# Loading a later block's x at the head of a block's steps instead of beside its row scatters

## The chip, the cores and the metric

The kernel runs on one core of a Trainium2 chip. Its time is the device time of one execution in microseconds; the time before is the median of three runs. Below, TensorE (PE) is the matrix engine, VectorE (DVE) and ScalarE (ACT) are the elementwise engines, GpSimd (POOL) issues indirect DMAs here, and SyncE (SP) issues plain DMAs. All DMAs are carried by the same 16 DMA engines of the core.

## The reference

The input x has 2 sequences of 4096 rows, 256 wide, in 32-bit floats. Two layers follow each other, both with a residual and a layer norm behind them.

```python
# layer 0: retention
q = (x @ Wq.T);  v = (x @ Wv.T)
state[t] = lam * state[t - 1] + v[t]          # along the sequence, lam by head
y = layernorm(q * state) * ln_g + ln_b
x = layernorm(x + (y * silu(x @ Wg.T)) @ Wo.T)
# layer 1: two of eight experts for each row
gates = softmax(x @ gate_W);  top two, scaled to sum 1 -> cw
out = x + sum_e cw[:, e] * (relu(x @ W1[e] + b1[e]) @ W2[e] + b2[e])
x = layernorm(out)
```

## The kernel before

The 8192 rows are taken in 16 blocks of 512 (`NB`). A block i passes through `attention(i)`, a generator whose `yield`s cut it into twelve steps: transposes of x, the projections v (with the scan that gives the state), g and q, the norm of y, the output product with the residual, the first layer norm (`x1`), the transposes of x1, the routing, and last the row scatters.

In the row scatters (L505) GpSimd issues eight indirect DMAs. Each sends 128 rows of x1, with their weights and row numbers, to a table `xs` in device memory that is ordered by expert, so that each row stands there twice. `schedule` then plans slots: 256 rows of one expert each, four for most blocks.

A slot is worked off in stages. `load_slot` (L605, SyncE) reads its rows as the tile xg. `slot_weights` (L619, L621, ScalarE) copies the expert's weights from `kept`. `slot_columns` (L632 on TensorE, L633 on VectorE) transposes xg. `slot_first` (L645 `ph`, L652 `hT`) and `slot_second` (L666 `po`, then L674 to L684 on VectorE, which make `to`, `weight` and `ysl`) are the two expert products. `store_slot` (L692, GpSimd) scatters the result rows to a table `ys`. When all slots of a group of blocks are stored, `load_sum` (L714) reads `ys` back, `weigh`, `scale_of` and `end` add the pairs and normalise, and `write_out` (L754) stores the output.

The two groups are 13 and 3 blocks long. The order of the instructions on TensorE, VectorE, ScalarE and SyncE is the order in which the program is written out (`IN_ORDER`), so it is set by the main loop (L836). In its turn i the loop advances the generators of blocks i - 2 (`older`), i - 1 (`old`), i (`new`) and i + 1 (`after`, its first step alone, the transposes of x_{i+1}). Between these steps `fill(n)` puts in slot work (`half`), loads of slots ahead (`load_ahead`, at most three) and, in turns 0 and 1, the loads of the experts' weights (`keep`, four DMAs an expert). The last `next(older)` of a turn holds the row scatters of block i - 2.

`load_x(i)` (L99 to L102) asks SyncE to load 512 KB into a tile of the ring `x` of five buffers. x_0 to x_2 are loaded at the start, x_{i+2} in turn i. The ring's buffer for x_{i+2} held x_{i-3}, which is read for the last time in turn i - 2 (L403). SyncE's queue is in order: a load of xg that waits for a free buffer (four of them, freed by L684) holds everything behind it.

Of the kernel before, what the change touches and what calls it, by code (L numbers as in the profile page):

```python
# [30 lines left out]
def kernel(  # L31
# [31 lines left out]
    NB = B * L // TB  # L63
# [27 lines left out]
    def wide_tile(name):  # L91
        wide_done.append(False)
        t = work.tile([P, NT, D], FP, tag="x", name=name, bufs=WIDE)
        return t, len(wide_done) - 1
# [4 lines left out]
    def load_x(i):  # L99
        t, k = wide_tile(f"x_{i}")  # L100
        nc.sync.dma_start(out=t, in_=xb[i])
        x_tiles[i] = t, k  # L102
# [42 lines left out]
    def keep(e, after):  # L145
        dma = nc.sync.dma_start(
            out=w2_sb[:, e, :, :], in_=w2[e].rearrange("(c p) d -> p c d", p=P)
        )
        if after is not None:
            tc.add_manual_dep(dma.ins, after, SYNC, reason="not all at once")  # L150
        at = 0
        for src, n in (
            (w1[e].rearrange("(c p) f -> p c f", p=P), NC),
            (b2[e : e + 1].partition_broadcast(P), 1),
            (b1[:, ts(e, NF)].unsqueeze(1), 1),
        ):
            size = n * src.shape[-1]
            nc.sync.dma_start(
                out=kept[:, e, at : at + size].rearrange("p (c f) -> p c f", c=n), in_=src
            )  # L160
            at += size
# [604 lines left out]
    def load_ahead():  # L766
        while slots and len(loaded) + len(ready) + len(turned) < 3:
            loaded.append(load_slot(slots.pop(0)))

    def turn_ahead():  # L770
        if not turned:
            weights_ahead()
        if ready and not turned:
            turned.append(slot_columns(ready.pop(0)))
# [21 lines left out]
    def half():  # L796

        turn[0] ^= 1
        done, size = 0, P
        if turn[0] or not hidden:  # L800
            load_ahead()
            turn_ahead()
            if turned:
                size = done = turned[0][4]
                weights_ahead()
                hidden.append(slot_first(turned.pop(0)))
        if not done and (len(hidden) == 2 or (hidden and not turned and not slots)):
            size = done = hidden[0][4]
            out_of.append(slot_second(hidden.pop(0)))
        elif out_of:  # L810
            store_slot(out_of.pop(0))
        load_ahead()
        turn_ahead()
        if not any(left.values()):
            return done

        todo = 3 * len(to_load) + len(to_weigh)
        debt[0] += todo * size / (P * max(1, 2 * sum(left.values()) - 8))
        some_combining(int(debt[0]))
        debt[0] -= int(debt[0])  # L820
        return done
# [14 lines left out]
    for i in range(NB + 2):  # L836

        now = sum(s[4] for s in slots + loaded) + sum(s[4] for s in ready + turned)
        now = 2 * min(5 * SL, now - SL * LAG * (i > FEW))

        def fill(n):
            nonlocal now
            if to_keep:
                keep(to_keep.pop(0), projected[0])
            load_ahead()
            for _ in range(n):
                done = 0
                while now > 0 and done < SL:
                    size = half() or SL
                    done += size  # L850
                    now -= size

        older, old, new, after = (
            steps[j] if 0 <= j < NB else iter(()) for j in (i - 2, i - 1, i, i + 1)
        )
        next(old, None)
        next(new, None)
        next(older, None)
        next(old, None)
        fill(1 if i > FEW else 0)  # L860
        next(new, None)
        next(old, None)
        if now > 0:
            turn_ahead()
        next(older, None)
        fill(1)
        next(new, None)
        fill(1)
        next(old, None)
        if 0 < i < NB - 2:  # L870
            load_x(i + 2)
        next(after, None)
        next(older, None)
        fill(1)
        next(old, None)
        fill(10)
# [57 lines left out]
```

## Time and profile before

| what | us |
|---|---|
| median of 3 runs | 1092.39 |
| lowest and highest run | 1091.66, 1093.06 |
| the profiled execution | 1088.11 |
| its span, first to last instruction | 1086.4 |
| TensorE busy in the span | 914.8 |
| VectorE busy | 623.1 |
| ScalarE busy | 389.7 |
| GpSimd busy | 339.7 |

The profile is of one execution. A page gives each engine's busy share in 40 slices of the span; with it go the clock that TensorE was granted (in tenths of full speed) and the busy share of the DMA engines. Other views list who waited for whom, the chain of waits that ended last, and the instructions of an engine in order of time; there, a number in brackets is the idle time before a row and the arrow names what ended it. "remote" and "another core or an unknown queue" stand where the profile finds no instruction that ended a wait in time. Queue q0 holds GpSimd's DMAs, q1 SyncE's, q8 and q14 the instruction fetches.

The x loads are issued at 0.9, 1.4, 2.0, 52.9, 54.3, 54.8, 124.7, 164.0, 232.4, 302.0, 356.9, 419.0, 476.5, 531.4, 588.9 and 643.2 us. The first transposes that read x_i start at 5.1, 33.2, 50.4, 76.0, 107.9, 143.2, 180.0, 238.3, 292.7, 347.5, 409.7, 467.1, 522.1, 579.5, 633.9 and 693.0 us. Row scatters of a block start at 80.6, 112.4, 147.9, 184.7, 243.0, 297.3, 352.2, 414.4, 471.8, 526.8, 584.2, 638.6, 697.7, 755.7, 810.0 and 856.8 us and take 9 to 10 us.

### The profile page before, as it was taken

Reading aid. Unit: us, or ns where it says so; the run is one execution under the profiler, and the core shown is the slowest. Engines: PE = TensorE matmul, PEld = TensorE weight load, DVE = VectorE, ACT = ScalarE, POOL = GpSimd, SP = SyncE. Lnnn points to the kernel's source line nnn. Section 1 sums busy time; section 2 is a strip of 40 time slices with the busy share of each in tenths; the row PEclk is TensorE's granted clock in tenths of the full one; section 3 lists DMA queues with packets and bytes.
Section 4 is the critical chain, followed back from the end, with each engine's and each line's share of the span. In section 5 each row is a group of like instructions: output and inputs, shape, how many; then the busy total and the mean of one; then the engine's idle time right before and its main releaser. Section 6 shows DMA issues by size and latency. Waiting matters only on the chain.

```text
span 1086.4 us, 15376 instructions
## 1 busy us (share of the span) xinstructions
PE 914.8 (84%) x4366; PEld 711.4 (65%) x4366; DVE 623.1 (57%) x2281; ACT 389.7 (36%) x825; POOL 339.7 (31%) x371
## 2 busy tenths in 40 slices
PE   3987879997989798989899998899979798668870
PEld 1554558775767677676767676667778687657760
DVE  1675766464656364656455655746373744667754
ACT  0221324323232232333332323143345453546652
POOL 3012341314151414141514141342433432333331
PEclk9998898998999899999999998999998999979995
DMA  6921221212030313031313121131212233657744
GB/s 206 329 77 41 70 65 61 84 40 79 20 119 21 101 38 99 21 100 40 103 36 97 43 96 43 51 109 46 79 51 84 86 115 113 184 172 219 227 138 174
DMA packets 63890, 105.33 MB, mean 97 GB/s; under 512 B 9616, under 2 KB 37552, under 8 KB 63552
## 3 DMA queue, kind: packets, MB, share of 16 engines
q1 hardware_dynamic: 47808, 62.21, 19.5%
q0 software_dynamic: 14320, 41.07, 10.3%
q10 hardware_dynamic: 1680, 1.06, 0.4%
q8 instruction: 38, 0.62, 0.2%
q14 instruction: 44, 0.36, 0.1%
HBM read 57.03 MB, written 49.44 MB: 98 GB/s over the span
## 4 chain that ended last, share of the span: by engine, by line
PE 56%; DVE 19%; DMA 9%; issue 4%; ACT 4%; another core or an unknown queue 3%; POOL 2%; SPq 1%; ACTq 0%; DVEq 0%; POOLq 0%
PE po L666 13%; PE ph L645 13%; DMA y<-ys 6%; PE q L314 5%; PE ao L399 5%; PE g L314 4%; PE ph_rest L645 4%; PE po_rest L666 4%; PE lg L423 3%; PE xt L632 2%; POOL xs L505 2%; DVE bnst_f L729 1%; DVE ysl L682 1%; DVE bnst_y L284 1%
## 5 line engine op out<-in xcount | busy, mean ns | idle before, releaser
L666 PE MATMUL po<-w_sb,hT 128*128 x800 | 201.4, 409 | 33.5 <-ACT hT L652 14.3
L666 PEld LDWEIGHTS po<-w_sb,hT 128*128 128x128 f32 x800 | 159.6, 205 | 63.3 <-ACT hT L652 15.7
L692 POOL DMA_INDIRECT ys<-ysl,to x100 | 97.7, 977 | 328.7 <-DVE ysl L684 303.5
L645 PE MATMUL ph<-xgT,w 128*128 128x256 f32 x800 | 185.2, 385 | 2.7 <-DVE xgT L633 2.2
L645 PEld LDWEIGHTS ph<-xgT,w 128*128 128x128 f32 x800 | 153.8, 194 | 28.8 <-issue 7.4
L652 ACT ACTIVATE hT<-ph,wb 128x256 f32<-128x256 f32 x200 | 81.5, 470 | 162.7 <-PE ph L645 100.8
L505 POOL DMA_INDIRECT xs<-x,pos x128 | 126.4, 987 | 38.7 <-issue 26.4
L645 PE MATMUL ph_rest<-xgT_rest,w_rest 128*128 128x128 f32 x672 | 87.4, 285 | 16.5 <-DVE xgT_rest L633 15.8
L645 PEld LDWEIGHTS ph_rest<-xgT_rest,w_rest 128*128 128x128 f32 x672 | 82.8, 198 | 24.6 <-issue 16.0
L666 PE MATMUL po_rest<-w_sb,hT_rest 128*128 x336 | 85.0, 398 | 14.4 <-issue 8.1
L682 DVE TENSOR_TENSOR ysl<-po,wb 128x512 f32<-128x512 f32 x50 | 34.4, 688 | 103.9 <-PE po L666 41.9
L633 DVE COPY xgT<-xt 128x512 f32<-128x512 f32 x50 | 34.5, 689 | 91.5 <-PE xt L632 64.3
L666 PEld LDWEIGHTS po_rest<-w_sb,hT_rest 128*128 128x128 f32 x336 | 62.6, 196 | 26.8 <-issue 12.2
L276 POOL TENSOR_TENSOR rstd_a<-rstd_a,half_neg 128x4 f32<-128x4 f32 x16 | 17.4, 1085 | 168.1 <-DVE at L490 112.8
L692 POOL DMA_INDIRECT ys<-ysl_rest,to_rest x42 | 41.8, 996 | 76.5 <-DVE ysl_rest L684 53.5
L314 PE MATMUL g<-xT,wg_sb 128*128 128x512 f32 x128 | 62.5, 634 | 3.8 <-DVE state L337 2.5
L652 ACT ACTIVATE hT_rest<-ph_rest,wb_rest 128x128 f32<-128x128 f32 x168 | 47.7, 363 | 42.9 <-PE ph_rest L645 28.2
L745 ACT ACTIVATE y<-y,less,rstd_f 128x256 f32<-128x256 f32 x64 | 34.8, 593 | 77.9 <-DVE less L740 77.9
L314 PE MATMUL q<-xT,wq_sb 128*128 128x512 f32 x128 | 60.4, 616 | 0.4 <-ACT yg L386 0.4
L314 PE MATMUL v<-xT,wv_sb 128*128 128x512 f32 x128 | 59.8, 611 | 0.3 <-issue 0.3
L399 PE MATMUL ao<-wo_sb,yg 128*128 128x256 f32 x256 | 58.2, 380 | 1.1 <-DVE y L361 1.1
L308 PE MATMUL pt_x<-ident,x 128*128 128x128 f32 x256 | 38.8, 285 | 21.9 <-DVE state L337 11.2
(164 smaller groups left out, 1319.3 us busy)
## 6 DMA issues: line engine op xcount, KB each, us to landing
y<-ys SPq DMA_DIRECT2D x32, 512.0 KB
xg<-xs SPq DMA_DIRECT2D x50, 264.0 KB
x<-in_x_dram SPq DMA_DIRECT2D x16, 512.0 KB
out_dram<-y SPq DMA_DIRECT2D x32, 256.0 KB
xg_rest<-xs SPq DMA_DIRECT2D x42, 132.0 KB
w_sb<-in_w_dram SPq DMA_DIRECT2D x8, 512.0 KB
kept<-in_w_dram SPq DMA_DIRECT2D x8, 512.0 KB
xs<-no_rows POOLq DMA_DIRECT2D x16, 132.0 KB
```

Of the source, the lines that this page charges most:

```text
L308: nc.tensor.transpose(pt[:, ts(t, P)], src[:, t, ts(c, P)], ident)
L314: last = nc.tensor.matmul(ps, w[:, c, ts(o, P)], xT[:, c, :], start=(c == 0), stop=(c == NC - 1))
L399: nc.tensor.matmul(o_ps[:, u, :], yg[:, c, ts(2 * t2 + u, P)], wo_sb[:, c, :], start=(c == 0), stop=(c == NC - 1),)
L423: nc.tensor.matmul(lg_ps[:, t, :], x1T[:, c, ts(t, P)], gw_sb[:, c, :], start=(c == 0), stop=(c == NC - 1),)
L505: gr.put(nc.gpsimd.indirect_dma_start(out=gr.xs, out_offset=bass.IndirectOffsetOnAxis(ap=pos[:, k, t, :], axis=0), in_=x1s[i][:, t, :], in ...
L633: nc.vector.tensor_copy(xgT, pt)
L645: nc.tensor.matmul(ph[:, u, :], w1_t[:, c, ts(f0 + u, P)], xgT[:, c, :], start=(c == 0), stop=(c == NC - 1),)
L652: nc.scalar.activation(hT[:, f, :], ph[:, u, :], AF.Relu, bias=b1_t[:, f : f + 1])
L666: nc.tensor.matmul(po[:, t, :], hT[:, f, ts(t, P)], w2_sb[:, ds(e, 1), f, :], start=(f == 0), stop=(f == NF - 1),)
L682: nc.vector.tensor_tensor(y, po, b2_t.broadcast_to([P, n_t, D]), ALU.add)
L692: gr.store(nc.gpsimd.indirect_dma_start(out=gr.ys, out_offset=bass.IndirectOffsetOnAxis(ap=to[:, t, :], axis=0), in_=y[:, t, :], in_offset ...
L745: nc.scalar.activation(z, z, AF.Identity, bias=less[:, t, :], scale=r[:, t, :])
```

## The change

`load_x(i + 2)` moves up in the loop's turn: from just before `next(after)` (and so before the step with the row scatters) to behind the first two steps, ahead of every `fill` of the turn.

```diff
         next(old, None)
         next(new, None)
+        if 0 < i < NB - 2:
+            load_x(i + 2)
         next(older, None)
         next(old, None)
         fill(1 if i > FEW else 0)
...
         next(new, None)
         fill(1)
         next(old, None)
-        if 0 < i < NB - 2:
-            load_x(i + 2)
         next(after, None)
         next(older, None)
         fill(1)
```

On SyncE the load of x_3 thereby stands ahead of the last twelve weight DMAs, those of x_7 and x_8 ahead of one load of xg, and those of x_9 to x_15 ahead of two (the third and the fourth of the block's four). The instructions of the other engines keep their order.

## The prediction

> **What bounds the kernel now.** I read the page first, then what SyncE's queue waits for, then who waits for x, then the chain of waits and TensorE's timeline around the scatters.
>
> The page:
>
> ```profile
> PE   3987879997989798989899998899979798668870
> PEclk9998898998999899999999998999998999979995
> DMA  6921221212030313031313121131212233657744
> PE 56%; DVE 19%; DMA 9%; issue 4%; ACT 4%; another core or an unknown queue 3%; POOL 2%; SPq 1%; ACTq 0%; DVEq 0%; POOLq 0%
> ```
>
> From 60 to 780 us TensorE is busy 80 to 90% of each slice and carries most of the chain; the DMA engines are 10 to 30% busy. The moved loads all run in that stretch. The answers on SyncE's waits, and on the tile x on SyncE:
>
> ```profile
> SPq L605 <- DVE ysl L684: 484.0, 44, 24.3
> ...
> L101 SPq DMA_DIRECT2D x<-in_x_dram x16: 372/436/1094, 0.9 to 643.2; - x16
> ...
> who waited for it (us, times):
>   PE pt_x L308: 5.1, 1
> ```
>
> SyncE is held 484 us by free xg buffers, so the loads stand far apart; the only wait for an x load in the whole run is the first, 5.1 us at the start. SyncE's timeline from 230 to 430 us:
>
> ```profile
> 232.39 0.44 SPq L101 DMA_DIRECT2D x<-in_x_dram  x1
> 255.07 46.89 SPq L605 DMA_DIRECT2D xg<-xs  x4
> 302.00 0.43 SPq L101 DMA_DIRECT2D x<-in_x_dram  x1
> 313.31 43.54 SPq L605 DMA_DIRECT2D xg<-xs  x4
> ```
>
> The load at 302.00 falls into POOL's eight row scatters (297.34 to 307.4), the one at 232.39 does not (243.0 to 253.1). After the scatters something is lost; the chain of waits and TensorE's timeline (idle time before the row, and its releaser, in brackets):
>
> ```profile
> 303.28 8.27 another core or an unknown queue
> 361.54 8.10 another core or an unknown queue
> ...
> 769.48 3.34 another core or an unknown queue
> ```
>
> ```profile
> 312.32 0.66 PE L632 MATMUL xt<-ident,xg 128*128 128x128 f32 x4 [2.27 <-DVE ysl L682]
> 370.62 0.79 PE L666 MATMUL po<-w_sb,hT 128*128 x1 [4.57 <-ACT hT L652]
> 431.00 1.47 PE L666 MATMUL po<-w_sb,hT 128*128 x3 [2.42 <-ACT hT L652]
> 769.53 1.78 PE L666 MATMUL po<-w_sb,hT 128*128 x7 [2.13 <-ACT hT L652]
> ```
>
> VectorE and ScalarE sit until a matmul result that TensorE's own rows put earlier (po ends at 306.59, its reader starts at 311.57). Then TensorE itself idles 2 to 5 us. This is the only place where the change can save anything.
>
> **The change part by part.** Compute engines keep their instruction order; only SyncE's queue changes. Thirteen loads are concerned, x_3 to x_15. Three (x_4 to x_6) keep their place in the queue.
>
> x_3 goes ahead of 12 weight DMAs of three experts. These are issued from 45.14 to 52.25 us; x_3 puts one issue (0.44 us) and its transfer before them. Their first reader, ScalarE's copy of w1 (L619), starts at 128.2 us, x_3's at 76.0 us. Bounds: zero, or one transfer (1.4 us, worked out below) if the first matmuls on x_3 came that early. I take 0.
>
> x_7 and x_8 go ahead of one xg load, x_9 to x_15 ahead of two. None of the seven carries a wait in its new place: their buffers were released a block earlier. They go out directly behind the block's second xg load, at 259.7 instead of 302.0, at 319.0 instead of 356.9, and so on, some 40 us earlier. Behind each on SyncE stand two xg loads that wait for VectorE some 20 us longer anyway (the third of the block goes out at 284.7 and 341.2): 0.44 us of issue costs nothing. If that cover were gone: 7 x 0.44 = 3 us.
>
> *The new place.* The load lands beside the second xg load and a pair of result scatters (L692, such as 318.36 and 319.63). The trace has that meeting once: x at 232.39, behind an xg load at 232.02, beside L692 at 231.78 and 233.13. There the 16 DMA engines were full from 234.5 to 236, and TensorE did not stop:
>
> ```profile
> 234.43 0.60 PE L632 MATMUL xt<-ident,xg 128*128 128x128 f32 x4
> 234.87 3.40 PE L399 MATMUL ao<-wo_sb,yg 128*128 128x256 f32 x15
> ```
>
> So 0. The upper bound is one transfer shown to TensorE each time: 512 KB at the 377 GB/s of the window below is 1.4 us, 7 x 1.4 = 9.7 us; the lower bound is zero, for nothing there waits for x now.
>
> A rule speaks against the move here. The Trainium skill, "DMA: Bandwidth & Descriptors", section "Issuing engines are not separate DMA queues", says that DMAs from SyncE and GpSimd run on the same 16 engines and interleave, so the collision is only moved, from eight row scatters to an xg load and two result scatters. By the rule the xg load or the pair would land up to one transfer later at the new place and the eight scatters earlier at the old one; by the row at 232 neither costs, since no instruction waits on them.
>
> *The old place.* Taking x out of the burst frees the DMA engines for a while. The window 304.5 to 305.5 us by queue (share of 16 engines):
>
> ```profile
> q1 hardware_dynamic: 361, 0.37, 103.9%
> q0 software_dynamic: 5, 0.01, 2.2%
> ```
>
> The scatters (q0) get almost nothing in that microsecond. But GpSimd paces them: the first and the eighth row scatter start 9.1 us apart with x (297.34, 306.44) and without it (243.01, 252.12).
>
> What TensorE loses in the seven bursts with x: idle gaps of 2.27, 4.57, 2.42, 2.33, 2.43, 1.57 and 2.41, together 18.0 us. By the trace's clock records the granted clock also falls to half in four of them: 6.83 us in the block 347.5 to 409.7, and 3.41 us in the blocks from 409.7, 522.1 and 633.9. That is 17.1 us at half clock, 8.5 us lost. The table of windows, one block each (columns: length, busy of PE, PEld, DVE, ACT, POOL, clock, DMA share, GB/s), shows it:
>
> ```profile
> 292.70:347.50 54.80, 50.42 (x238) 39.08 (x237) 31.95 (x115) 18.37 (x37) 17.85 (x18) 1.00 0.22 69
> 347.50:409.70 62.20, 55.10 (x238) 42.47 (x237) 32.32 (x115) 18.37 (x37) 17.86 (x18) 0.92 0.20 61
> ```
>
> Same instructions, 7.4 us apart: clock and gap. The best gain is all of it, 18.0 + 8.5 = 26.5 us. For the size I take bursts without x. Nearest is the one at 755.7: eight row scatters, then four result scatters, an xg load, no x. Its gap is 2.13 plus 0.48 us, so 7 x 2.6 = 18.3 us, no gain in gaps; its clock stays whole, which would save the 8.5. Its first matmul result (po) ends at 763.52 and is read by VectorE at 764.28, 0.8 us later; with x it is 5.0 us (306.59, 311.57) or 3.6 us (423.62, 427.2). A less alike burst, at 243, lost 6.72 us and 6.83 us at half clock. So relief in the clock is half seen: I take half of 8.5, 4.2, less 0.3 in gaps, 3.9 us saved. Bounds: 26.5 saved; or each burst at 6.83 us of half clock, 7 x 3.4 - 8.5 = 15.4 us lost.
>
> A rule weighed on the clock: the Trainium skill, "TensorE: Matmul & The Clock Gate", Part 1, has the half clock after an idle window of about 3.4 us. The row at 431.00 shows it after a gap of 2.42 us. By the rule only the 4.57 us gap would halve it, 3.4 us in all; by the rows it is 8.5.
>
> Sum: 0 + 0 + 0 - 3.9. The profiled execution took 1088.11 us, span 1086.4; it stands 4.3 us below the median 1092.39. Against itself 1084.2; carried to the median **1088.5 us**.
>
> **The rivals.** *Hidden anyway.* No one waits for x now, and scatters are paced by GpSimd; the waits after the burst stay, as they do at 769.48 in the chain without any x. Then 1092.4 us. Against it: the late 3.5 to 5 us that only bursts with x show on the first result.
>
> *Slower by the clock.* The gap after the burst stays, but lies otherwise against the windows of 3.41 us in which the clock is granted, and falls to half more often. For it: the gaps are alike (2.3 to 2.4 us) and three of six such met a half clock, three did not; the burst at 243, without x, met 6.83 us. Price: 1.7 us for each further 3.41 us, up to 15.4 us, 1107.8; it decides from two more windows on (3.4 us), 1095.8.
>
> *The load shows at its new place.* Up to 9.7 us, 1102; against it the row at 232 and the quiet DMA engines.
>
> **How the numbers follow.** Relief 0.46 (its own range 1066 to 1090), hidden 0.22, slower 0.32 (clock 0.24, new place 0.08). Two in ten are left outside 1076 to 1104: a relief of over 16 us needs nearly all gaps gone, a loss of over 11.5 us most of the bursts at the long half clock. The time is that of relief, 1088.5. About 0.2%, 2.2 us, is what a measurement of this kernel can tell from none: faster 0.46, same 0.22, slower 0.32.
>
> **What would show it.** In the changed profile: x loads at about 259.7, 319.0, 379.5 on SyncE, still no wait for x after the first; q0 no longer starved 7 us into the burst; the first result after the burst read 1 us late, not 5; fewer half-clock windows between 290 and 690 us. If the gaps of 2.3 us stay and the block lengths stay between 54 and 62 us, the old place was no cost. It is wrong if TensorE gains a wait in the first 10 us after a block's second xg load, or if the block lengths rise with the clock.

## The result and the profile after

The changed kernel takes 1089.83 us in the median of 20 runs, the kernel before, run beside it, 1090.28 us. The ratio is 1.0001 with a 95% interval of 0.9982 to 1.0019: the same. The single runs of each spread over more than 10 us (1085.89 to 1098.08 and 1079.47 to 1094.03). The median lies in the predicted range and 1.3 us from the predicted time, but what happened is the rival "hidden anyway" and not the relief that the forecast was made of.

The page of the changed kernel, which was profiled in an execution of 1092.28 us (span 1090.6):

```profile
PE   3987889897989898989898989898978798778870
PEclk9997889998999999999999999899889999979995
DMA  6931212302030312121212121312112233556744
PE 50%; DVE 23%; another core or an unknown queue 8%; DMA 8%; issue 4%; ACT 3%; POOL 2%; SPq 1%; ACTq 0%; DVEq 0%; POOLq 0%
```

From 290 to 690 us the granted clock has fewer dips, but "another core or an unknown queue" has grown from 3% to 8% of the chain (a second profile of the kernel before, below, has 8% too). The answers on tile x on SyncE, and SyncE's timeline:

```profile
L101 SPq DMA_DIRECT2D x<-in_x_dram x16: 3/435/648, 0.9 to 601.1; - x16
...
who waited for it (us, times):
  PE pt_x L308: 5.2, 1
  ACT w L619: 0.4, 1
```

```profile
261.49 0.00 SPq L101 DMA_DIRECT2D x<-in_x_dram  x1
286.48 35.51 SPq L605 DMA_DIRECT2D xg<-xs  x4
322.04 0.43 SPq L101 DMA_DIRECT2D x<-in_x_dram  x1
344.22 34.88 SPq L605 DMA_DIRECT2D xg<-xs  x4
```

The loads moved to where they were expected, 40 us earlier, and no engine waits for one after the start but ScalarE's copy of a weight tile, 0.4 us once. The chain of waits, and the timeline around the row scatters of 299.2 to 309.2 us, which now have no x beside them: TensorE first, then VectorE, ScalarE and GpSimd.

```profile
305.09 8.41 another core or an unknown queue
361.20 8.73 another core or an unknown queue
...
753.96 10.81 another core or an unknown queue
```

```profile
304.69 3.72 PE L666 MATMUL po<-w_sb,hT 128*128 x16 [0.85 <-issue]
308.24 3.62 PE L645 MATMUL ph<-xgT,w 128*128 128x256 f32 x16
314.27 1.12 PE L632 MATMUL xt<-ident,xg 128*128 128x128 f32 x4 [2.42 <-DVE ysl L682]
...
313.53 0.69 DVE L682 TENSOR_TENSOR ysl<-po,wb 128x512 f32<-128x512 f32 x1 [8.44 <-remote]
...
313.68 1.56 ACT L652 ACTIVATE hT<-ph,wb 128x256 f32<-128x256 f32 x4 [5.22 <-remote]
...
310.79 0.96 POOL L692 DMA_INDIRECT ys<-ysl,to  x1 [0.30 <-issue]
315.02 0.96 POOL L692 DMA_INDIRECT ys<-ysl,to  x1 [3.26 <-DVE ysl L684]
```

By TensorE's rows, po ends at 308.41. VectorE starts on it at 313.53, 5.1 us later, 1.8 us behind the last DMA that GpSimd issued without a pause (310.79 + 0.96). ScalarE is let go at about the same moment and runs all four `hT` without a wait. They need the sixteen matmuls `ph` that stand behind po, 3.62 us in TensorE's row; had TensorE itself stood until 313.5, they could not have been ready. The signals for po and the two halves of ph are recorded at 313.50, 313.59 and 313.69, while the rows put their ends 1.7 us apart (308.41, 310.13, 311.86). So TensorE had done the work; what is late is its signals. TensorE then idles 2.42 us. The seven gaps of this kind are 2.42, 2.73, 2.50, 2.43, 2.48, 2.40 and 2.52 us, 17.5 us; before they were 18.0. The table of windows, one block each (length, busy of PE, PEld, DVE, ACT, POOL, clock, DMA share, GB/s):

```profile
294.50:350.50 56.00, 51.63 (x237) 40.17 (x236) 32.05 (x115) 18.35 (x37) 17.85 (x18) 0.97 0.22 68
350.50:407.70 57.20, 52.17 (x238) 40.30 (x237) 32.14 (x115) 18.36 (x37) 17.86 (x18) 0.97 0.21 66
407.70:462.80 55.10, 50.43 (x237) 39.11 (x236) 32.09 (x115) 18.35 (x37) 17.86 (x18) 1.00 0.22 69
```

The seven blocks from the transposes of x_8 to those of x_15 take 390.4 us, 9.9 less than in the profile before (400.3). The next two take 95.1 and 61.8 us, where before had 88.8 and 57.5. Whether any of this belongs to the change was the first thing to ask.

### The profile page after: what moved, and what is told of

Its sections match the earlier page's. It is cut to its first block, busy times and chain, and to the rows that moved or that the text cites. A ratio compares the mean times of both kernels' runs of the same rounds, so it can differ in the third digit from the quotient of the medians.

```text
span 1090.6 us, 15377 instructions
## 1 busy us (share of the span) xinstructions
PE 916.7 (84%) x4366; PEld 713.1 (65%) x4366; DVE 623.1 (57%) x2281; ACT 389.0 (36%) x825; POOL 339.6 (31%) x371
## 4 chain that ended last, share of the span: by engine, by line
PE 50%; DVE 23%; another core or an unknown queue 8%; DMA 8%; issue 4%; ACT 3%; POOL 2%; SPq 1%; ACTq 0%; DVEq 0%; POOLq 0%
PE po L666 10%; PE ph L645 9%; DMA y<-ys 5%; PE q L314 5%; PE ao L399 5%; PE po_rest L666 4%; PE ph_rest L645 4%; PE g L314 4%; PE lg L423 3%; DVE ysl L682 2%; DVE bnst_a L284 2%; DVE ysl L684 2%; PE xt L632 2%; POOL xs L505 2%
## 5 line engine op out<-in xcount | busy, mean ns | idle before, releaser
L666 PE MATMUL po<-w_sb,hT 128*128 x800 | 197.1, 402 | 26.1 <-ACT hT L652 9.3
L666 PEld LDWEIGHTS po<-w_sb,hT 128*128 128x128 f32 x800 | 156.8, 201 | 54.4 <-issue 12.1
L645 PEld LDWEIGHTS ph_rest<-xgT_rest,w_rest 128*128 128x128 f32 x672 | 84.1, 201 | 26.9 <-issue 13.6
L666 PE MATMUL po_rest<-w_sb,hT_rest 128*128 x336 | 87.4, 407 | 14.0 <-issue 8.2
```

What stands on the lines that cost most here:

```text
L645: nc.tensor.matmul(ph[:, u, :], w1_t[:, c, ts(f0 + u, P)], xgT[:, c, :], start=(c == 0), stop=(c == NC - 1),)
L666: nc.tensor.matmul(po[:, t, :], hT[:, f, ts(t, P)], w2_sb[:, ds(e, 1), f, :], start=(f == 0), stop=(f == NF - 1),)
```

## Experiments

Three series were run, each on one chip: A (the kernel before takes 1088.17 us there), B (1036.57) and C (1081.52). Ratios are to the kernel before in the same series. The result above is of a chip that is near A in time (1090.28).

**The kernel before, profiled again (series A).** No edit.

> The kernel before, profiled a second time. Theory 'hidden anyway': the load beside the row scatters costs nothing, and the 10 us between the seven blocks with x in the burst (first transposes of x_8 to those of x_15: 400.3 us before, 390.4 us after) are half-clock windows that fall differently in each execution. Then this execution has the seven blocks somewhere between 388 and 402 us, and the long blocks are not those of the first profile (62.2 us for the second of the seven). Theory 'gained and given back': the seven blocks are worth 10 us and the same 10 us are lost behind them. Then this execution again has 398 to 402 us there, with the second block over 60 us.

It took 1094.13 us (span 1092.5). The table of windows:

```profile
293.70:350.40 56.70, 52.11 (x238) 40.25 (x237) 31.95 (x115) 18.37 (x37) 17.84 (x18) 0.97 0.22 67
350.40:405.80 55.40, 50.41 (x237) 39.09 (x236) 32.13 (x115) 18.36 (x37) 17.87 (x18) 1.00 0.22 68
```

The block that took 62.2 us in the first profile takes 55.4. The seven blocks take 392.2 us, the next two 95.1 and 61.8: like the changed kernel, not like the first profile of its own. The 9.9 us that seemed gained, and the 10.6 that seemed given back, differ between two profiles of the same kernel. (The chip of the first profile is not on record, so part of this may lie between chips.)

**No x in the burst at all (series A, and again in C).** In the kernel before, x_9 to x_15 are not loaded; blocks 9 to 15 compute on x_8.

```diff
+        if i > 8:
+            x_tiles[i] = x_8
+            return
```

> x_9 to x_15 are not loaded at all; blocks 9 to 15 compute on x_8 (so the output of these blocks is that of other rows). All 3.5 MB of x traffic beside seven bursts of row scatters are gone; every engine's instructions stay. 'Hidden anyway': within 0.3% of before; TensorE's gap behind each burst stays at 2.3 to 2.7 us, the first po after the burst is still read 3.5 to 5.4 us late. 'Gained and given back': the seven blocks take about 390 us, the total 4 to 10 us less than before, as nothing is put elsewhere. 'Relief' as predicted: 3.9 us less.

It took 1091.31 us, ratio 1.0048 (1.0009 to 1.0087): no gain. Its timelines, TensorE and VectorE:

```profile
300.70 3.72 PE L672 MATMUL po<-w_sb,hT 128*128 x16 [0.82 <-issue]
...
309.61 0.69 DVE L688 TENSOR_TENSOR ysl<-po,wb 128x512 f32<-128x512 f32 x1 [8.50 <-remote]
```

The result is read 5.2 us late (304.42, 309.61) with no x transfer anywhere in the stretch. Taken between po's end by TensorE's rows and its signal in the trace, the seven bursts are late by:

| kernel, series A but "before, first profile" and "after" | us late, seven bursts |
|---|---|
| before, first profile (x in the burst) | 4.96 3.14 3.53 5.01 3.52 4.25 3.52 |
| before, second profile (x in the burst) | 5.16 5.46 5.21 5.17 5.16 5.16 5.12 |
| after (x at the new place) | 5.10 5.41 5.19 5.11 5.16 5.08 5.20 |
| no x | 5.16 5.41 5.08 5.12 5.12 5.17 5.10 |
| four times the x traffic in the burst | 5.10 5.44 5.67 5.39 5.50 5.56 5.55 |

The first profile of the kernel before is the least late, with x; its spread of 3.1 to 5.0 comes back in series C without x (3.5 to 5.3, below). x does not make the result late, so taking it away could not relieve anything.

> x_9 to x_15 are not loaded at all and blocks 9 to 15 compute on x_8, once more. Theory (x's transfer hides at either place): within 0.3% of the kernel before, so the 1.0048 measured first was of the spread. Rival (taking x away costs something real): 1.004 or more again. Rival (relief): 0.997 or less.

In series C the same kernel had 0.9963 (0.9931 to 0.9996). The two intervals don't meet: an interval from one series on one chip says less than it seems to.

**Four times the traffic, at the old and at the new place.** Behind each load of x_9 to x_15 three more copies of the same 512 KB go into spare device memory, in one kernel at the old place of the load, in the other at the new one.

```diff
             load_x(i + 2)
+            if i >= 7:
+                spare_loads(i + 2)
```

> The kernel before with three more copies of 512 KB (x to a spare table in device memory) right behind each of the seven loads x_9 to x_15, at the old place beside the row scatters: four times the traffic there. 'Hidden anyway': within 0.3% of before, unless the copies hold the next xg load (12 us away) or the scatters' rows. If x beside the scatters costs anything, three more cost about three times as much: at the 3.9 us of the prediction 12 us slower (1.1%), at the 10 us of the one profile 30 us (2.7%).

> The changed kernel with the same three copies of 512 KB behind each of the seven loads, at the new place behind the block's second xg load. 'Hidden anyway': within 0.3% of before. 'The load shows at its new place' (up to 1.4 us for one transfer): three more show 7 x 3 x 1.4 = 29 us, 2.7% slower.

In series A the old place cost 1.0106 (1.0059 to 1.0152), 1094.27 us, and the new place 1.0038 (1.0004 to 1.0071), 1090.08 us. By the ratios that is 11.5 and 4.1 us for 21 copies. In the profile of the old place the late result is 0.3 to 0.5 us later in five of seven bursts and TensorE's gaps are 2.4 to 3.0 us instead of 2.4 to 2.7, together some 2 us; where the rest was is not located.

> The old place with three more copies of the same 512 KB behind each of x_9 to x_15, once more. In the first run it cost 1.0106, and its profile has the po result behind the burst seen 5.4 to 5.7 us late where the changed kernel has 5.1 to 5.4. Theory (the x traffic costs only through the late signals of the burst): on a chip without late results within 0.3% of the kernel before; on one with them 1.006 to 1.015 again. Rival (the traffic itself costs): 1.006 or more on a chip without late results too.

In series C the old place had 0.9974 (0.9937 to 1.0010): no cost. So the extra traffic has no price that both series show.

**The two parts of the change alone (series B).**

```diff
-        if 0 < i < NB - 2:
+        if 7 <= i < NB - 2:
             load_x(i + 2)
...
+        if 0 < i < 7:
+            load_x(i + 2)
```

> Only x_9 to x_15 move to the head of the block's steps; x_3, x_7 and x_8 stay at their old place. Theory (hidden anyway, both parts): within 0.3% of the kernel before, since the run with no x_9 to x_15 at all was not faster (1.0048) and the profile after has the same TensorE gaps of 2.4 to 2.7 us behind the row scatters. Rival (two parts that cancel): the late loads give a relief of 4 us or more (0.9965 or less) that the early ones give back; then this run is faster than before by over 0.3%. Rival (the reverse): slower by over 0.3%, the early loads gaining.

> Only x_3, x_7 and x_8 move; x_9 to x_15 stay beside the row scatters. Theory (hidden anyway): within 0.3% of the kernel before; x_3 ahead of twelve weight DMAs costs at most one transfer, 1.4 us (0.13%). Rival (two parts that cancel): slower by 4 us or more (1.0035 or more), with the first blocks up to x_8's transposes longer in the profile. The two halves together should come to the 1.0001 of the whole change.

The late loads alone: 1035.66 us, 0.9993 (0.9982 to 1.0005). The early ones alone (the two conditions exchanged): 1035.94 us, 0.9994 (0.9984 to 1.0004). In this series neither does anything, so nothing cancels. It spreads little (the kernel before 1033.42 to 1038.37). But its profiles, those of the two halves among them, have no late result (the next run shows one), so there was nothing here that the late loads could have relieved: for the relief the table above speaks, and these two runs only show that the new places cost nothing.

**The changed kernel, again (series B and C).** No edit.

> The changed kernel again, for a second profile. Theory (the 10 us between the two first profiles in blocks 8 to 15, 400.3 against 390.4 us, are of the execution, not of the change): the stretch from x_8's to x_15's transposes is again 389 to 393 us, as in the second profile of the kernel before (392.2), and the two stages behind it again 95 and 62 us. Rival (the change does shorten the blocks and lengthens what follows): 390 us here too, but then the second profile of before should have had 400, which it had not; a value of 397 or more here would show that both kernels vary.

It took 1034.43 us, span 1032.8, some 58 us less than the same program in its first profile. The seven blocks take 369.1 us, the next two 85.6 and 52.8, below what either theory gave. This series has no late results, as the following lines show. The page's chain, TensorE's and VectorE's timeline, and two windows:

```profile
PE 56%; DVE 25%; DMA 10%; issue 3%; ACT 2%; POOL 2%; SPq 1%; ACTq 0%; POOLq 0%; DVEq 0%
```

```profile
289.00 3.72 PE L666 MATMUL po<-w_sb,hT 128*128 x16 [0.86 <-DVE xgT L633]
292.56 3.62 PE L645 MATMUL ph<-xgT,w 128*128 128x256 f32 x16
296.01 0.60 PE L632 MATMUL xt<-ident,xg 128*128 128x128 f32 x4
...
292.76 0.69 DVE L682 TENSOR_TENSOR ysl<-po,wb 128x512 f32<-128x512 f32 x1 [3.35 <-PE po L666]
```

```profile
384.50:438.20 53.70, 51.68 (x238) 40.36 (x237) 32.28 (x115) 18.48 (x37) 17.83 (x18) 0.97 0.22 71
438.20:490.20 52.00, 49.97 (x238) 39.16 (x237) 32.21 (x115) 18.47 (x37) 17.85 (x18) 1.00 0.23 73
```

"Another core or an unknown queue" is gone from the chain. Eight row scatters run from 283.45 to 293.5 us and four result scatters follow without a pause, yet po, which ends at 292.72, is read at 292.76, and TensorE goes on without a gap. No result of TensorE is seen over 0.4 us late in this whole profile. A block takes 52.0 us, or 53.7 with one half-clock window.

> The changed kernel, timed again beside the others of this call. Theory (hidden anyway): within 0.3% of the kernel before on either sort of chip; the two halves of the change gave 0.9993 and 0.9994. Rival (the relief of the burst exists but drowns in the spread of the first sort): on a chip without late results 0.997 or less.

In series C, 1077.41 us and 0.9949 (0.9917 to 0.9981). There the results are late again: VectorE reads po 4.2 to 5.2 us after its end in the seven bursts, and 3.5 to 5.3 us in the same series without x. The kernel without x (0.9963) and the one with four times the x traffic at the old place (0.9974) came out on the same side, so x's place does not explain the 0.5%; what does is open.

**Four more scatters (series B, and again in C).** GpSimd issues twelve indirect DMAs in each block instead of eight; the four go to a spare table. The expectations call the base the changed kernel without x in the burst; it is the kernel before, with x beside the scatters, and the ratio is to that.

```diff
+        for t in range(2):
+            for k in range(2):
+                spare_put(gr, nc.gpsimd.indirect_dma_start(
+                    out=gr.spare,
+                    out_offset=bass.IndirectOffsetOnAxis(ap=pos[:, k, t, :], axis=0),
+                    in_=x1s[i][:, t, :],
```

> The changed kernel with four more indirect DMAs by GpSimd behind each block's eight row scatters, into a spare table that nothing reads; x is not in the burst. Theory (TensorE's gap behind the burst belongs to the scatters themselves): the first po result that VectorE reads late, by 5.1 to 5.4 us in the profile after, is read late until the longer burst ends, so later by up to 4 x 1.27 = 5 us in each of 16 bursts, the gap of 2.4 us grows, and the time rises by 16 x 2 to 16 x 5 = 32 to 80 us (1.03 to 1.07). Rival (the gap is set by something that ends by itself, as the order of the steps): the gaps stay 2.4 us, and only GpSimd's result scatters behind the burst go out later; the time rises by less than 1%.

In series B: 1060.05 us, 1.0228 (1.0211 to 1.0246), with no result late. The 23.5 us lie in the first blocks: the stretch up to the transposes of x_8 grows from 278.8 us (of the changed kernel in this series) to 305.5, and the seven blocks take 369.0 as against 369.1. What waits in those first blocks is not shown.

> The changed kernel with four more indirect DMAs by GpSimd behind each block's eight row scatters, once more. In the first profiles (span 1086 to 1093 us) TensorE's results become visible 1.7 to 1.9 us behind the last DMA of GpSimd's burst, some 5.1 us late; in the profiles at 1033 to 1059 us none is late. Theory (GpSimd's burst of DMAs holds up TensorE's signals, on some chips only): if the profile is of the first sort, the po result behind the burst is again seen 1.6 to 1.9 us behind the burst's last DMA, so up to 5 us later than 5.1, TensorE's gap grows with it and the time rises by clearly more than the 1.0228 measured before, 1.05 or more. If the profile is of the second sort: 1.02 again, none late. Rival (the lateness has a length of its own): 5.1 us late as without the four, and about 1.02 on either sort.

In series C: 1184.51 us, 1.0963 (1.0917 to 1.1008), 103 us more, over four times the cost of series B. The chain; TensorE, VectorE, ScalarE and GpSimd in one burst; and two blocks:

```profile
401.18 13.36 another core or an unknown queue
```

```profile
406.85 0.66 PE L646 MATMUL xt<-ident,xg 128*128 128x128 f32 x4 [2.28 <-DVE ysl L696]
415.51 4.71 PE L680 MATMUL po<-w_sb,hT 128*128 x11 [8.00 <-ACT hT L666]
...
406.11 0.69 DVE L696 TENSOR_TENSOR ysl<-po,wb 128x512 f32<-128x512 f32 x1 [8.30 <-remote]
...
414.71 0.69 DVE L647 COPY xgT<-xt 128x512 f32<-128x512 f32 x1 [7.00 <-remote]
414.62 1.57 ACT L666 ACTIVATE hT<-ph,wb 128x256 f32<-128x256 f32 x4 [13.44 <-remote]
...
406.05 0.96 POOL L514 DMA_INDIRECT spare<-x,pos  x1 [0.31 <-issue]
...
411.39 0.96 POOL L706 DMA_INDIRECT ys<-ysl,to  x1 [0.31 <-issue]
```

```profile
322.50:387.20 64.70, 52.57 (x238) 40.52 (x237) 32.02 (x115) 18.37 (x37) 21.70 (x22) 0.92 0.21 67
387.20:452.00 64.80, 52.49 (x237) 40.57 (x236) 32.16 (x115) 18.36 (x37) 21.98 (x22) 0.92 0.21 67
```

The pieces of the chain are 13.3 us here and 8.4 in the profile after, apart by the 5 us that four scatters, 1.27 us each, add to the burst. VectorE now sits twice, and TensorE loses 8.00 us on top of 2.28: the seven blocks take 453.7 us, 9.4 each more than the changed kernel's 388.0 in this series. (The stretch ahead of them grows by 33.3 us, in series B by 26.7; the seven blocks, which lost nothing there, lose 65.7 here.)

The time went as the theory expected, but po itself did not: in six of the seven bursts it is read 4.3 to 5.6 us late (7.1 in the other), about as without the four scatters (4.2 to 5.2), which is what the rival said, and GpSimd goes on issuing (406.05) while it is read (406.11). The burst's length shows on the results behind po: ScalarE reads the first half of ph 11.7 to 11.8 us late in all seven, where the changed kernel in this series has 3.3 to 3.6, and the signals come 2.2 to 2.5 us behind the burst's last DMA (412.35, 414.53), a little more than the 1.6 to 1.9 expected. So the lateness grows with the number of scatters, in a series that has it at all; but a pause of GpSimd is not the only thing that lets a result through, and what else does is not shown.

## Why the prediction was right and wrong, step by step

**Compute order kept, only SyncE's queue moves; loads at 259.7, 319.0, 379.5.** Right: 261.5, 322.0 and 379.1, and no new wait behind them.

**The early loads at 0.** Right, in series B: 0.9994 for x_3, x_7 and x_8 alone.

**The new place at 0.** Right: from 258 to 700 us TensorE has no idle time that a load of x ends, and in the 20 us behind the load at 322.04 its gaps are 0.44 and 0.48 us. The bound of 9.7 us was far off; three more copies of the same size there, 21 in all, came to 4.1 us in series A.

**"0.3 us lost in gaps".** Near: 18.3 us of gaps were forecast, 17.5 came, where the two profiles of before have 18.0 and 17.7. But the row that gave the 18.3 does not stand for a burst without x, as the next step shows.

**"With x it is 5.0 us", without it 0.8: the first result read 1 us late, not 5.** This is the step that failed. The 0.8 us came from one burst without x, at 755.7 us, and from its first result alone. A few rows further in the same burst VectorE waits for the transposes xt, which end at 767.41 in TensorE's rows, until 772.90, 5.5 us late and still without x:

```profile
772.90 0.69 DVE L633 COPY xgT<-xt 128x512 f32<-128x512 f32 x1 [7.01 <-remote]
```

In the profile after, po is read 2.3 us late in that same burst and xt 5.7 us (the 10.81 us in the chain at 753.96). In series C its po is again 0.8 us late in the changed kernel and in the one without x, while the seven bursts have 3.5 to 5.3 us: the 0.8 belongs to that burst and not to the missing x. Without any x the seven bursts of series A are late by 5.1 to 5.4 us. So the price of a burst without x was read too low: 1 us was forecast, 5 came. The choice of row was the error. The other burst without x in that profile, at 243 us, had its first result 2.2 us late (252.27, 254.43) and 6.72 us of idle TensorE; it was called less alike and set aside, and it was the one that spoke. In the profile after all seven late results come 1.7 to 1.9 us behind the last of GpSimd's DMAs, as without x; the run with twelve scatters, where po comes while they go on, shows that this pause is not the whole of it.

**"q0 no longer starved" 7 us into the burst.** True, and worth nothing. The share by queue at the same distance into the burst, 306.4 to 307.4 us, of the changed kernel:

```profile
q0 software_dynamic: 42, 0.12, 31.9%
q8 instruction: 1, 0.02, 7.5%
```

The scatters move as they are issued (q0 had 2.2% before), but the eight are still issued over 9.1 us, so the burst is no shorter.

**"4.2 us saved by half of the half-clock loss".** Wrong as a cause. By all clock records of the seven blocks the first profile of before had 23.9 us at half clock (the prediction counted 17.1 and missed windows later in two blocks), the changed kernel has 10.2. That would be 6.8 us saved; but the kernel before had 13.6 in its second profile. Most of the difference lay in that one profile and not in the change. The prediction took the sum of one profile for a property of the kernel, though its own execution stood 4.3 us from the median.

**The rule on idle windows and half clock,** which the prediction weighed against its rows: the rows were read too simply as well. In series B half-clock windows of 3.41 us fall at 317.6, 423.4 and 580.5 us, in blocks where no idle time of TensorE is over 0.92 us, and each costs 1.7 us (53.7 against 52.0). A gap of 2.4 us is not what it takes, nor an idle window of 3.4 us; what stands ahead of the one at 317.6 is 0.48 us of idle time and sixteen matmuls with eight columns of output (L423, from 314.59).

**The rivals.** "Hidden anyway" gave 1092.4 us and the condition "the waits after the burst stay, as they do at 769.48 without any x". That is what the runs show, and 0.22 was too little for it. "Slower by the clock" did not come: 5.1 us lost at half clock in the seven blocks after, 6.8 in the repeat of before. That the time was close is luck: the two terms of the forecast were small, and it was set 3.9 us below a median of three runs, 1092.39, where twenty runs give 1090.28. The change that was forecast, 3.9 us, did not come; the medians differ by 0.45 us.

What remains open: the 0.5% in series C, which the kernel without x shows too; why series B has no late results (each series was of one chip, so the chip and the occasion can't be told apart); and what holds TensorE's signals during the burst and lets some through before it ends.

## What to carry to other kernels

Before an idle gap is put down to the transfer that lies in it, look at every like place without that transfer, the least convenient first: here one such place showed a result 0.8 us late and another 6.7 us of idle TensorE, and the wrong one was taken. A profile is one execution: read the unchanged kernel twice before a difference of 10 us in one stretch is given a cause, and where series on several chips differ by more than their intervals, trust the sign that repeats. Look also past the first row of such a place: the results behind it in the same burst were 5.5 us late. A long unbroken run of indirect DMAs on GpSimd went with late results of TensorE in two of three series, and a longer one made them later; so its length, not its company on the DMA engines, is the thing to try to shorten. No run here shortened it.

## What the runs showed of the hardware that was not expected

- The same program takes 1034 us on one chip and 1077 to 1092 us on others. The 57.8 us between the profile after and that of series B are 15.7 up to the transposes of x_8, 21.3 in the seven blocks, 18.5 in the next two stages and 2.3 in the rest. In the slower chips' profiles of the kernels without the four scatters TensorE's results po, ph and xt are read up to 7.8 us late in GpSimd's bursts; the faster one has none over 0.4 us. What is late is the signal, not the work: three signals come within 0.19 us for work that TensorE's rows spread over 3.45 us (308.41 to 311.86).
- Four more scatters a block cost 23.5 us on the chip without late results and 103 us on one with them.
- In the trace such a wait shows as "remote" or "another core or an unknown queue", on a kernel of one core: it is a signal of TensorE that comes later than the row that should have sent it.
